# Traced rates for a build-time planner, sums placed later, and a 5x5 layer that alternates between sample and quarter-image inputs

## The chip, the cores and the metric

The kernel runs on one core of a Trainium2 chip. The metric is the device time of one execution in microseconds (us), given as the median of several runs. Engines are named as in the profile: PE (TensorE matmul), PEld (its weight loads), DVE (VectorE), ACT (ScalarE), POOL (GpSimd), SP (the queue that issues most DMAs).

## The reference, cut to what matters

Four layers, each `x = x + layer(groupnorm(x))`, on x of 16 samples, 32 channels, 128 x 128, float32.

```python
x = x + L0(_gn(x), ...)   # a row-skewed LSTM that scans over 128 columns
x = x + L1(_gn(x), w)     # quantised; out[f] = -sum over channels and 3x3 taps of |patch - w|
x = x + L2(_gn(x), w1)    # 2-D Hartley transform, 32x32 modes mixed over channels, transform back
x = x + L3(_gn(x), ...)   # U-net, below
# L3: five edge operators, each normalised per sample -> 160 channels
#   conv1 3x3 (160->32), maxpool2, conv2, maxpool2, conv3, maxpool2, conv4,
#   deconv1+conv5, deconv2+conv6, deconv3+conv7, times the input
```

In L1, 32 filters in 8 sets of 4, times 9 taps, are 72 differences for each half of each sample. In L3 the five operators and conv1 are folded into one 5x5 convolution whose weights depend on the sample's statistics.

## The kernel before, in words

**Stage 0** (to 687 us) is L0. It isn't changed.

**Stage 1** (687 to 5609 us) is L1, class `Differences`. It walks 16 samples x 2 halves, 32 units in all; each unit is 72 differences. One difference is either `nc.scalar.activation(Relu)` on ACT (L757, tile `d_act`, two buffers) or `nc.vector.tensor_scalar` on DVE (L760, tile `d_dve`, three buffers). PE then sums it over channels with 16 matmuls (`sums`, L647), tap by tap into four PSUM banks. `linear` (L662) adds nine more terms, `keep_busy` (L677) issues matmuls with zero weights where the plan has a gap, and `finish` (L628, L630) takes the unit out and its statistics.

**Behind it** the work of L2 and L3 is woven in. It runs on groups of four samples (class `After`): `forward` (transform, L1110 to L1082, then `mixing`, L1221), `back` (L1295, L1345), `statistics` (Gram products, L1487, and the operators' norms, L1555), the weights `wf` from tables `v` (L1610 to L1625), `conv1` (the sides, L1837, then eight chunks of 25 taps x 16 matmuls, L1863), `small_layers` (conv2, conv3, conv4, L1661; upsampling, `Composed.round`, L908 and L934), and `last`. Group g may start only when stage 1 has finished sample 4g+3.

**The order is made at build time.** `Weave` keeps a planned clock for PE, DVE and ACT. Each step of a generator yields its PE time in us; `yield SUMMED` waits until the plan has PE done with it, and `yield -x` waits x us. After every difference, `weave.advance(due)` issues background steps while they start before the next sum is due:

```python
            start = max(self.pe, self.ready)
            if start + 1.0 > due + SLACK:
                return
```

The planner also chooses ACT or DVE for each difference, and `keep_busy` fills what it thinks is left. `keep_order` then fixes this order on every engine; nothing is decided at run time. So a wrong price shows as an engine that waits, with all that stands behind it in its queue.

**The tail** (5609 to 6606 us): when the 72 x 32 differences are issued, `drain` runs what is left of the weave beside a second one for group 3. Group 3 keeps its image in SBUF (`whole`). `drain` steps whichever weave is behind in planned time.

**Layouts that the change touches.** In `conv1` a chunk is 16 image rows, `xp` of 20 rows with the halo; the four row tiles j of PE take four rows each (4j + kh). The output `y1` is `padded`: one image per channel. Each PE output bank holds, on partitions 32j to 32j+31, row tile j, so `spread` takes a bank out with four instructions of 32 partitions. A `quartered` tile holds a quarter of the image rows for each block of 32 partitions, so that `evict` takes a bank out with one instruction of 128 partitions; `neighbours` then copies the halo rows between the quarters.

## Time and profile before

| | |
|---|---|
| median of 3 runs | 6603.08 us (6602.0 to 6603.86) |
| the profiled execution: its time, its span | 6607.96 us, 6606.2 us |
| stage 0; stage 1; tail | 687 us; 4922 us; 997 us |
| busy over the span: PE, DVE, ACT | 81%, 84%, 82% |
| granted PE clock, mean | 0.919 |
| differences: on ACT, on DVE | 626 x 7148 ns, 1678 x 2360 ns |

The profile's groups give, for each line, engine and tile, the count, the busy time, the mean of one, and the idle time that its engine had just before it with what ended it. The windows give the busy time of every engine in a stretch, with the granted clock. In the profile each float32 matmul stands as two records, so that a 5x5 chunk of 400 matmuls is 800 records. A busy PE isn't one at its peak: ends of matmuls are modelled.

### The profile page before, as it was taken

The numbers are of one execution on the slowest core, as the hardware profiler recorded it, in microseconds if no ns is written. First come the engines' busy times: TensorE is split into PE (matmuls) and PEld (weight loads), VectorE is DVE, ScalarE is ACT, GpSimd is POOL, SyncE is SP. The second block draws the span as 40 slices with busy tenths as digits, with TensorE's granted clock in tenths as the row PEclk, the third lists the DMA queues.
The fourth block names the chain that finished last, engine by engine and source line by source line (L and its number), as shares of the span: only waits on it lengthen the run. The fifth ranks groups of instructions, "written<-read, shape, count | busy, mean of one in ns | idle before, by whom it ended". The sixth has DMA issues, their size and how long they took to land.

```text
span 6606.2 us, 269623 instructions
## 1 busy us (share of the span) xinstructions
PE 5331.0 (81%) x126486; PEld 2789.1 (42%) x126486; DVE 5543.3 (84%) x6844; ACT 5422.6 (82%) x3179; POOL 70.0 (1%) x67
## 2 busy tenths in 40 slices
PE   3798677788777879997887769998877779888796
PEld 3676233333334433333333433333333433445584
DVE  7898899999999989998899999999999999233322
ACT  3898899999999999998999989999999999112112
POOL 0000000000000000000000000000000000000000
PEclk9999899999998989998999889999999889987798
DMA  7553322221253632211553642121553641422302
GB/s 315 216 188 116 78 57 62 54 54 46 59 155 107 200 96 59 70 45 42 121 154 91 210 133 61 49 63 37 124 151 89 194 137 34 155 76 73 85 4 64
DMA packets 360800, 681.08 MB, mean 103 GB/s; under 512 B 71236, under 2 KB 219716, under 8 KB 348804
## 3 DMA queue, kind: packets, MB, share of 16 engines
q1 hardware_dynamic: 352212, 629.41, 33.3%
q0 software_dynamic: 7040, 33.80, 1.5%
q8 instruction: 989, 16.20, 1.0%
q14 instruction: 127, 1.04, 0.1%
q10 hardware_dynamic: 432, 0.64, 0.0%
HBM read 481.00 MB, written 182.69 MB: 100 GB/s over the span
## 4 chain that ended last, share of the span: by engine, by line
issue 33%; PE 29%; DVE 18%; ACT 15%; DMA 4%; SPq 1%; POOL 0%; DVEq 0%; ACTq 0%; POOLq 0%
PE acc L1863 11%; DVE d_dve L760 11%; ACT d_act L757 10%; PE acc L647 8%; PE pg L223 3%; PE acc L908 2%; PE acc L1661 2%; ACT gt L237 2%; DVE y L1768 1%; ACT junk L198 1%; DVE stat L124 1%; DMA xm_d<-xm 1%; DMA x_in<-in_x_dram 1%; DVE pooled L1757 1%; DMA v<-fold_d 1%
## 5 line engine op out<-in xcount | busy, mean ns | idle before, releaser
L757 ACT ACTIVATE d_act<-q,neg 128x8192 f16<-128x8192 f16 (+1 forms) x626 | 4428.1, 7148 | 159.2 <-PE acc L647 132.3
L760 DVE TENSOR_SCALAR d_dve<-q,qw 128x8192 f16<-128x8192 f16 (+1 forms) x1678 | 3871.1, 2360 | 174.4 <-PE acc L647 154.6
L647 PE MATMUL acc<-d_dve,sel 128*32 128x512 f16 x26848 | 1871.4, 401 | 445.5 <-DVE d_dve L760 346.8
L647 PEld LDWEIGHTS <-sel 128*32 128x32 f16 x36864 | 1003.6, 100 | 2088.2 <-issue 1416.4
L647 PE MATMUL acc<-d_act,sel 128*32 128x512 f16 x10016 | 728.0, 412 | 313.8 <-ACT d_act L757 299.3
L1863 PE MATMUL acc<-xp,wf 32*32 32x512 f32 x19200 | 757.3, 614 | 16.1 <-issue 12.9
L1771 ACT ACTIVATE y<-pooled,b 32x128 f32<-32x128 f32 x456 | 182.4, 400 | 429.9 <-DVE pooled L1757 423.7
L677 PE MATMUL acc<-q,zero 128*32 128x512 f16 x5676 | 407.2, 398 | 0.5 <-issue 0.5
L1863 PEld LDWEIGHTS acc<-xp,wf 32*32 32x32 f32 x19200 | 257.1, 104 | 324.9 <-issue 277.3
L223 PE MATMUL pg<-h,wb 64*64 64x20 f32 (+15 forms) x8192 | 345.9, 308 | 54.4 <-DVE h L251 29.5
L908 PE MATMUL acc<-y,u_conv 32*32 32x256 f32 (+1 forms) x9984 | 332.9, 447 | 68.0 <-issue 50.1
L237 ACT ACTIVATE gt<-pg,bias 128x20 f32<-128x20 f32 (+15 forms) x1024 | 332.7, 385 | 40.2 <-PE pg L223 37.8
L223 PEld LDWEIGHTS pg<-h,wb 64*64 64x64 f32 x8192 | 255.3, 153 | 129.9 <-DVE h L251 77.0
L677 PEld LDWEIGHTS <-zero 128*32 128x32 f16 x5676 | 169.6, 101 | 156.4 <-issue 31.5
L908 PEld LDWEIGHTS acc<-y,u_conv 32*32 32x32 f32 x9984 | 154.4, 109 | 190.7 <-issue 142.3
L1898 DVE TENSOR_TENSOR acc<-acc,cut 128x4 f32<-128x4 f32 x256 | 36.0, 164 | 227.8 <-PE acc L1863 225.3
L1863 PE MATMUL acc<-image,wf 32*32 32x512 f32 x6400 | 218.7, 599 | 0.6 <-issue 0.4
L223 PE MATMUL pg<-xn,wb 64*64 64x2 f32 (+63 forms) x4096 | 186.9, 293 | 25.5 <-issue 17.2
L1661 PE MATMUL acc<-y,w_conv 32*32 32x512 f32 (+2 forms) x4608 | 172.2, 528 | 37.0 <-issue 18.5
L1487 PE MATMUL acc<-xp 32*64 32x204 f32 (+2 forms) x6432 | 180.1, 337 | 26.1 <-issue 26.0
L1994 ACT ACTIVATE xr<-xr,l_ms 128x1024 f32<-128x1024 f32 x48 | 51.6, 1147 | 164.8 <-DVE xr L2024 110.8
L1863 PEld LDWEIGHTS acc<-image,wf 32*32 32x32 f32 x6400 | 169.7, 103 | 37.9 <-issue 8.7
(247 smaller groups left out, 3994.5 us busy)
## 6 DMA issues: line engine op xcount, KB each, us to landing
q<-q_d SPq DMA_DIRECT2D x128, 536.2 KB, 9.9
x_in<-in_x_dram SPq DMA_DIRECT2D x16, 2048.0 KB, 14.7
xn<-in_xs_dram SPq DMA_DIRECT2D x64, 512.0 KB, 7.1
res<-in_x_dram SPq DMA_DIRECT2D x64, 512.0 KB, 8.9
x_d<-res SPq DMA_DIRECT2D x64, 512.0 KB, 5.0
xq<-x_d SPq DMA_DIRECT2D x256, 128.0 KB, 4.1
xr<-x_d SPq DMA_DIRECT2D x256, 128.0 KB, 4.9
x_d<-xr SPq DMA_DIRECT2D x256, 128.0 KB, 2.6
```

The source lines that it names most:

```text
L124: nc.vector.bn_stats(stat0[:, g, 8 * q + k, :], t[:, k * 512 : (k + 1) * 512])
L223: nc.tensor.matmul(bank[c][q][64 * pair : 64 * pair + 64, :, :width], wb[half, 4 * kind + KIND[q]].rearrange("p b o -> p (b o)"), v[half], ...
L237: nc.scalar.activation(gt[:, q, :, :n], bank[c][q][:, :, :n], AF.Tanh if q == G else AF.Sigmoid, bias=bias[:, KIND[q] : KIND[q] + 1],)
L647: self.nc.tensor.matmul(acc[k][32 * j : 32 * j + 32, :], self.sel16[:, i // 9, :], d[:, row : row + 4, c : c + W], start=first, stop=last,)
L677: self.nc.tensor.matmul(acc[k][32 * j : 32 * j + 32, :], self.zero, q[:, :4, :W], start=False, stop=False)
L757: nc.scalar.activation(dst, src, AF.Relu, bias=self.neg[:, i : i + 1])
L760: nc.vector.tensor_scalar(dst, src, self.qw[:, i : i + 1], 0.0, ALU.subtract, ALU.max)
L908: nc.tensor.matmul(acc[blk][32 * j : 32 * j + 32, o : o + rows * n], t[part, 4 * par + tap, :], own[:, top : top + rows, left : left + n], ...
L1487: nc.tensor.matmul(gram[blk][j : j + width, at : at + n], xp[part, l, 2 + j : 2 + j + width], xp[part, rows, j : j + width + 4], start=sta ...
L1661: nc.tensor.matmul(acc[blk][32 * j : 32 * j + 32, : rows * n], wc[name][part, tap, :], src[part, at : at + rows, kw : kw + n], start=tap == 0,
L1771: nc.scalar.activation(d, s, AF.Identity, bias=bj)
L1863: nc.tensor.matmul(acc[blk][32 * j : 32 * j + 32, :], tap_of("all", tap)[rows], xp[rows, 4 * j + kh : 4 * j + kh + 4, kw : kw + W], start= ...
```

## The change

**Planner constants.** `PE_US` (one sum) 1.0 to 0.88, `SLACK` 3.0 to 1.0, a new `ACT_SPARE` of 1.5 us by which a sum of an ACT difference is placed later, the price of `linear` 0.45 to 0.36 and that of a `keep_busy` block 0.25 to 0.22. Every step's yield is set anew.

**Layout.** For groups 0 to 2 the 5x5 layer no longer reads the image chunk by chunk. `window(ch)` holds, for each of the four image quarters, eight rows starting at row 4 ch of that quarter; row tile j works in quarter j. The windows are loaded again from the padded image in DRAM, one DMA each. `y1` and `y3` become quartered, and conv1, conv2, conv3 and conv4 are taken out with one instruction per bank. Two additions for the image's left and right edge become one.

**Buffers.** Frames grow from 20 to 32 rows; to make room, the tables `gm` go from 5 to 3 buffers and `v` from 4 to 3 for groups 0 to 2, frames of the last weave from 4 to 3, and the DMA scratch from 4096 to 2048.

```diff
-DVE_US, ACT_US, PE_US = 2.36, 7.15, 1.0
-LATE = 1.5
-SLACK, CLOCK = 3.0, 1.0
+DVE_US, ACT_US, PE_US = 2.36, 7.15, 0.88
+LATE, ACT_SPARE = 1.5, 1.5
+SLACK, CLOCK = 1.0, 1.0
...
-        for k in range(min(int((until - start - 0.1) / 0.25), 4)):
+        for k in range(min(int((until - start - 0.1) / 0.22), 4)):
...
-                    unit["late"].append((ends[act], i, act, t))
+                    unit["late"].append((ends[act] + (ACT_SPARE if act else 0.0), i, act, t))
...
-            yield rows * n / 512 * 0.2 + 0.95        # Composed.round, one tap
+            yield rows * n / 512 * 0.78 + 0.28
...
-        self.buffers = {..., "frames": 2, "gm": 5, "e_v": 4, "l_x": 2}
+        self.buffers = {..., "frames": 2, "gm": 3, "e_v": 3, "l_x": 2}
...
-            yield 1.0                                # mixing
+            yield 0.3
             if ky % 4 == 3 and 8 < ky < M1 - 1 and not weave.draining:
-                yield -2.5
+                yield -5.5
...
-                    yield 1.1                        # back, first step
+                    yield 0.35
...
-                yield 0.8                            # back, second step
+                yield 0.4
...
-        ring = [pool.tile([128, 20, W + 4], F32, name=f"xp{i}") for i in range(self.buffers["frames"])]
+        ring = [pool.tile([128, 32, W + 4], F32, name=f"xp{i}") for i in range(self.buffers["frames"])]
...
-        def again(ch, half):
-            own = slice(10 * half, 10 * half + 10)
-            nc.sync.dma_start(chunk(ch)[:, own, :], padded(ch, own.start, own.stop))
+        def again(ch):
+            t = self.d["xn"]
+            rows = bass.AP(
+                t.tensor, t.offset + g * 128 * PADDED + 4 * ch * PW, [[PADDED, 128], [32 * PW, 4], [1, 8 * PW]]
+            )
+            nc.sync.dma_start(window(ch).rearrange("p (q r) w -> p q (r w)", q=4), rows)
...
-                yield 0.5                            # statistics, one row
+                yield 0.38
...
-            y1 = self.padded(y1p, 64, "y1")
+            y1 = self.quartered(y1p, 64, "y1")
...
-                            xp[rows, 4 * j + kh : 4 * j + kh + 4, kw : kw + W],
+                            xp[rows, at + apart * j + kh : at + apart * j + kh + 4, kw : kw + W],
...
-                yield 1.15                           # conv1, one tap
+                yield 1.06
...
-                for s, col in enumerate((0, W - 1)):
-                    nc.vector.tensor_tensor(a4[:, :, col], a4[:, :, col], cut[:, blk, s, ch, :], ALU.add)
+                nc.vector.tensor_tensor(sides_of, sides_of, both, ALU.add)
...
-                    self.spread(lambda part, j: y1[part, top + 2 * j : top + 2 * j + 2, 1:65], out[blk], blk, ...)
+                    self.evict(y1[:, blk, 1 + 2 * ch : 3 + 2 * ch, 1:65], out[blk], b1[:, blk : blk + 1], blk, nc.scalar)
+                if ch in (0, 7):
+                    self.neighbours(y1, 16, ch == 7, ch == 0)
...
-    nc = bacc.Bacc("TRN2", target_bir_lowering=False, num_devices=1, dynamic_dma_scratch_size=4096)
+    nc = bacc.Bacc("TRN2", target_bir_lowering=False, num_devices=1, dynamic_dma_scratch_size=2048)
```

Here `apart, at` are `8, 0` for a window and `32, 4 * ch` for the kept image of group 3. conv2 runs as two halves over the taps 3 to 8 and then 0 to 2, so that the halo rows from the last chunk are needed only for the last three.

## The prediction

> **What bounds the kernel now.** I read the page's head and slices first, then windows over the two stages that the change touches, then the waits inside stage 1, and last the groups, for prices.

> ```profile
> span 6606.2 us, 269623 instructions
> PE 5331.0 (81%) x126486; PEld 2789.1 (42%) x126486; DVE 5543.3 (84%) x6844; ACT 5422.6 (82%) x3179; POOL 70.0 (1%) x67
> ...
> DVE  7898899999999989998899999999999999233322
> ACT  3898899999999999998999989999999999112112
> ```

> The page's rows for DVE and ACT fall from 9 to 2 at slice 35. Up to there the kernel is stage 1; behind it is another machine. The windows price both:

> ```profile
> 687.00:5609.00 4922.00, 4041.58 (x88090) 1870.70 (x88091) 4677.28 (x3941) 4745.19 (x1180) 59.63 (x45) 0.93 0.35 94
> 5609.00:6607.00 998.00, 818.67 (x26105) 537.45 (x26087) 304.02 (x853) 163.10 (x327) 7.94 (x15) 0.87 0.27 76
> ```

> Columns: length, busy time of PE, PEld, DVE, ACT, POOL, then granted clock, DMA share and GB/s. In stage 1 DVE and ACT are busy 95% and 96%; less work on both, or less waiting, is what shortens it. In the tail PE is busy 82%, DVE 30%: PE and the chain of waits bound it. A second cut shows what PE does there:

> ```profile
> 5612.00:6250.00 638.00, 515.55 (x15566) 297.83 (x15564) 214.09 (x595) 92.76 (x187) 7.94 (x15) 0.83 0.35 98
> 6250.00:6607.00 357.00, 300.12 (x10473) 238.52 (x10468) 89.44 (x258) 67.45 (x134) 0.00 (x0) 0.93 0.14 38
> ```

> At 6250 group 2's last matmul is done; group 3 runs alone after it. The same windows for line L1863 alone (PE, PEld, clock, DMA):

> ```profile
> 5612.00:5887.00 275.00, 190.31 (x4704) 78.28 (x4704) 0.91 0.46 136
> 6250.00:6432.00 182.00, 181.84 (x5568) 151.78 (x5564) 1.00 0.06 16
> ```

> A chunk is 800 records. So six chunks of group 2's conv1 lie in the tail before 5887, and alone a chunk costs 182/5568 x 800 = 26.1 us. In the waits of stage 1 the sums (L647) and the differences wait for each other:

> ```profile
> PE acc L647 <- DVE d_dve L760: 346.8, 318, 10.3
> PE acc L647 <- ACT d_act L757: 299.3, 185, 6.1
> PEld acc L1863 <- issue: 223.9, 533, 3.1
> DVE d_dve L760 <- PE acc L647: 154.6, 115, 8.6
> ACT d_act L757 <- PE acc L647: 132.3, 47, 19.8
> ```

> The two last rows cost time: 155 us of DVE and 132 us of ACT, because PE had not yet freed a buffer. PE's own waiting costs nothing by itself, but a sum that waits for ACT holds the DVE sums queued behind it.

> [...] its clock has only two values, and one sum's 16 matmuls, which take 1.05 us at 1154 us, take 1.90 us at 1165.9, after PE had waited 2.54 us; the mean in stage 1 is 0.93. [...] a DVE take-out that is placed too early blocks the differences behind it, as `ta` (L1114) does here, up to 5.25 us.

> **The change part by part.** Counts come from the two programs' orders of instructions, durations from the groups of this execution.

> *1. The layout takes work off ACT and DVE in stage 1.* ACT: 280 take-outs of 32 partitions go, 88 of 128 come. [...] L1771's 400 ns agrees. So -280 x 0.40 + 88 x 0.40 = -77 us. The planner gives ACT 631 differences for 626: +5 x 7.15 = +36. ACT's sum: **-41 us**. DVE: 128 take-outs of conv2 to conv4 become 32, -96 x 0.275 = -26; 144 edge additions of 164 ns become 88, -9; 16 more poolings (0.66) +11; 27 halo copies at 0.2 (estimate, from 128x16 copies of 0.175 and 128x128 of 0.284) +5; five differences fewer, -12. DVE's sum: **-31 us**. These lie on the engines that set stage 1, so it can shorten by 30 to 40 us.

> *2. The background runs ahead.* Cheaper yields let `advance` issue more between two sums. In units of 72 differences, the order of before starts group 2's transform at unit 27.2 and its conv1 at 31.0; the order after at 26.0 and 29.1. At the end 2400 of its conv1 matmuls (six chunks) lay behind the last difference, afterwards 511 (1.28): **4.72 chunks leave the tail**. The price of before, 1.15 us a tap, was above the 1.05 that the lone chunk shows; 1.06 is true. PE pays for them in stage 1, 4.72 x 26.1 = 123 us, and for 2908 more zero matmuls, at most 157 us (16 per 0.86 us); it was busy 82% there, so 90% after. Nothing on DVE or ACT is added by this beyond part 1.

> *3. What the tail saves.* If PE alone counted: 123 us, 150 where the chunks shared PE (275 us for 5.88 chunks, with other work between). If group 3's waits alone counted: nothing. So I went through group 3 by steps, taking from the trace each step's own PE time and waits, and from the order after what is left of group 2 to fill them. Start to first transform: 51 us before, 45 after. Transform 55, 45. Wait for modes and mixing 94, 53 (14 us of PE idle is before it now; conv2 and conv3 cover it). Trip through z and L1295: 81, 55. L1345: 71, 55. Statistics' lead 37, 35. Statistics up to group 2's new end 60 and their rest, alone, 45 (125 in all before). Weights 38, 38. Sides 34, 20. These are 586 before and 451 after. Conv1 from there: 238 before (its first chunk shared PE with group 2), 217 after. What follows it, 170 before: four take-outs, each shorter by 1 to 2 us, give 164. Sum: 994 to 832, -162. I take **-150 us**, since less filler means more half clock (0.56 already at 6150 to 6200) and waits that I can't see. Range -100 to -175.

> *4. Waiting in stage 1.* SLACK 1.0 lets a background step make a sum late by one step, where before it was three us; with three buffers DVE has 2 x 2.36 - 0.88 = 3.8 us before it notices. ACT's sums placed 1.5 us later spare PE part of the 299 us; the ACT buffer still has 7.15 - 1.5 - 0.88 us to spare. More zeros hold the clock: 118 of the 220 us that DVE idles lie at half-clock stretches. Against it, the true rates leave no margin when the clock halves, and take-outs come due earlier. I take **-35 us**, between -120 and +70.

> *5. Fewer table buffers.* With `v` at 3 and `gm` at 3, a reload is issued after a use and needed three uses later. [...] here `v` lands in 6.9 us (median) and `gm` in 7.2, so the trace's numbers are used. `v` is used every 1.4 us where steps come in a row, so perhaps one wait of 4 us in each group; `gm` is used every 2.6 us, so one of 3 us. DVE would hold the differences behind it. Three groups: **+20 us**, 0 to 60 (the smaller DMA scratch, which no row prices, is in the upper end).

> *6. At nothing.* Window loads: 24 of 2.1 MB for 48 of 0.66 MB. A load of 2 MB lands in 14.7 us (x_in), and a chunk lasts 65 us of stage 1 (0.42 units of 154 us), so two windows cover it. In the tail a chunk lasts 26 us: still covered. q, xq and xr queue behind it on SP, with about 20 us of lead each. The layout of conv matmuls: same counts and shapes.

> **Sum.** -31 (DVE's side) - 150 - 35 + 20 = -196 us: 6606 to about 6410 for a profiled span. The median of the runs stands 3 us below that span: **6407 us**.

> **Rivals.** *Hidden gain lost:* late take-outs and table waits eat part 1 and 4, and only the tail shortens, less the table waits; 6603 - 150 + 20 = 6473; 0.18. For it: the removed price margin. Against it: PE still has about 10%. *Waits vanish:* DVE idles 100 us instead of 220, 6407 - 90 = 6317; 0.12. For it: up to 1500 us DVE idles next to nothing (2 us of 313 in 687 to 1000), as zeros alone fill PE there. *The tail doesn't shrink:* group 3's chain sets it, -30 there, 6527; 0.05. Against it: PE at 515 of 638 us. *Slower:* PE becomes the bound of stage 1. If the half clock meets the denser order, sums fall behind by more than the 3.8 us of buffers, DVE and ACT stand, and each of the 24 units that carry background grows. The gain of 150 + 31 is used up at 7.5 us a unit (5%); at 9 us the time is 6603 - 181 + 216 = 6638; 0.06. For it: the conv1 stretch goes from 3.71 to 3.41 units in group 0. Against it: that stretch runs at clock 0.95 to 0.98, PE's own work there is near 90%. That the change doesn't do what it says is excluded for the order, not for its effect.

> **How the numbers follow.** The likeliest case has 0.59, about 6360 to 6450. With the rivals, 6315 to 6510 leaves out 2 in 10. 0.2% (13 us) is about what a measurement of this kernel can tell from no change: the tail's case splits 0.03 to faster and 0.02 to same, so faster 0.59 + 0.18 + 0.12 + 0.03 = 0.92, same 0.02, slower 0.06.

> **What the new profile would show.** Last difference at 5540 to 5600 us, tail of 830 to 880 us; under 1100 records of conv1's `xp` after it; L1771's group at a quarter of its instructions, still about 400 ns; waits of d_dve for L647 under 155 us; granted clock of stage 1 at or over 0.93. I am wrong if stage 1 ends after 5609, or if PE's share of the tail drops below 75%, which would mean that waits took the place of the chunks.

## The result, and the profile after

The changed kernel takes **6502.38 us** (median of four runs, 6494.89 to 6506.94), the kernel before 6603.47 us beside it on the same chip: ratio 0.9845, interval 0.9828 to 0.9862. That is 101 us faster, about half of the 196 us that the prediction's sum gave. The time lies inside the range of 6315 to 6510 us that the prediction named, 8 us from its upper end, and outside its likeliest case of 6360 to 6450. That was luck in part: the range was wide because of the rivals, and the sum that it was built around was off by a factor of two. The profiled execution took 6506.94 us with a span of 6505.2; the one of before has 6606.2, so the two spans differ by 101 us too and can be compared piece by piece.

The head, the slices and the chain of work that ended last, from the page of the changed kernel:

```profile
span 6505.2 us, 274662 instructions
PE 5343.1 (82%) x129394; PEld 2805.1 (43%) x129394; DVE 5475.0 (84%) x6551; ACT 5312.8 (82%) x2816; POOL 65.6 (1%) x67
...
DVE  7799899999999999999999889999989889744212
ACT  3899799999999989999999899999989899702001
...
PE 41%; issue 25%; DVE 20%; ACT 8%; DMA 4%; SPq 1%; POOL 0%; DVEq 0%; ACTq 0%; POOLq 0%
```

DVE and ACT have lost 68 and 110 us of work over the whole span, as the layout should bring. But between slices 22 and 33 DVE's row now has five 8s and ACT's three, where those of before have none and one. PE's share of the last chain is 41%; before it was 29%. Work went off DVE and ACT, and PE has become what they wait for more often.

Windows over stage 1 and the tail of the changed kernel (length, busy time of PE, PEld, DVE, ACT and POOL, granted clock, DMA share, GB/s):

```profile
691.00:5646.00 4955.00, 4224.36 (x94756) 1948.29 (x94757) 4654.82 (x3827) 4708.23 (x999) 55.25 (x45) 0.94 0.36 99
5646.00:6506.00 860.00, 651.62 (x22340) 478.61 (x22336) 258.17 (x673) 90.50 (x144) 7.97 (x15) 0.83 0.30 81
```

Length less busy time gives idle time. The tail is 138 us shorter (998 to 860). Stage 1 is 33 us **longer** (4922 to 4955), although DVE is busy 22 us less in it (4677 to 4655) and ACT 37 us less (4745 to 4708): DVE's idle time rose from 245 to 300 us, ACT's from 177 to 247. Stage 0, which is unchanged, took 4 us more in this execution. So 4 + 33 - 138 = -101.

The waits in stage 1 of the changed kernel (total us, times, longest):

```profile
PE acc L647 <- DVE d_dve L760: 333.6, 327, 31.3
...
DVE d_dve L760 <- PE acc L647: 195.1, 191, 10.6
ACT d_act L757 <- PE acc L647: 190.1, 86, 13.1
PE acc L647 <- ACT d_act L757: 142.4, 100, 4.5
```

Before, these read 346.8, 154.6, 132.3 and 299.3. PE waits 157 us less for ACT, and DVE and ACT wait 98 us more for PE. Read together, the two say that PE runs later than it did; the prediction took the first half of that as a gain and missed the second.

Two stretches of 450 us show some of where. First the kernel before, in group 1's conv1 and then in group 2's transform, mixing, transform back and statistics:

```profile
4000.00:4450.00 450.00, 432.29 (x9528) 166.33 (x9524) 426.46 (x286) 438.98 (x175) 0.00 (x0) 0.97 0.23 62
4900.00:5350.00 450.00, 351.29 (x8128) 187.92 (x8116) 430.70 (x373) 446.43 (x110) 15.00 (x9) 0.91 0.51 146
```

The corresponding stretches of the changed kernel lie 150 us earlier:

```profile
3850.00:4300.00 450.00, 432.98 (x9869) 162.23 (x9862) 428.96 (x266) 434.43 (x94) 0.00 (x0) 0.99 0.25 70
4750.00:5200.00 450.00, 350.71 (x8708) 189.55 (x8700) 401.42 (x417) 407.56 (x111) 17.56 (x15) 0.89 0.53 159
```

In group 1's conv1 PE is busy 96% of the stretch, and DVE idles no longer than before (24 us, then 21). In the other stretch PE is busy 78% in both kernels, and DVE's idle time goes from 19 to 49 us, ACT's from 4 to 42.

These two don't stand for the whole of stage 1. In the changed kernel group 2's conv1 fills its last 416 us; there PE is busy 97% and DVE idles 28 us:

```profile
5230.00:5646.00 416.00, 404.62 (x9374) 158.44 (x9368) 388.42 (x224) 397.69 (x79) 0.00 (x0) 0.99 0.20 57
```

Cut into pieces of 50 us (mean over five places of the cuts), the pieces of stage 1 in which PE is busy 93% or more hold 56 us of DVE's idle time before and 87 us after. So about half of the 55 us lies where PE is fullest, and the rest where it has time free. Little of it lies at half clock: 94 us of DVE's idle time fell there before, 102 after.

### The profile page after: what moved, and what is told of

The parts are those of the page before. It is cut to its first block, busy times and chain, and to the rows that moved or that the text cites. A ratio compares the mean times of both kernels' runs of the same rounds, so it can differ in the third digit from the quotient of the medians.

```text
span 6505.2 us, 274662 instructions
## 1 busy us (share of the span) xinstructions
PE 5343.1 (82%) x129394; PEld 2805.1 (43%) x129394; DVE 5475.0 (84%) x6551; ACT 5312.8 (82%) x2816; POOL 65.6 (1%) x67
## 4 chain that ended last, share of the span: by engine, by line
PE 41%; issue 25%; DVE 20%; ACT 8%; DMA 4%; SPq 1%; POOL 0%; DVEq 0%; ACTq 0%; POOLq 0%
PE acc L647 14%; PE acc L1874 13%; DVE d_dve L760 12%; ACT d_act L757 4%; PE acc L908 3%; PE pg L223 3%; ACT gt L237 2%; PE acc L1664 2%; ACT junk L198 1%; PE acc L1491 1%; PE acc L677 1%; DVE stat L124 1%; PE acc L662 1%; DMA v<-fold_d 1%; PE acc L1221 1%
## 5 line engine op out<-in xcount | busy, mean ns | idle before, releaser
L757 ACT ACTIVATE d_act<-q,neg 128x8192 f16<-128x8192 f16 (+1 forms) x631 | 4470.2, 7149 | 209.1 <-PE acc L647 190.1
L760 DVE TENSOR_SCALAR d_dve<-q,qw 128x8192 f16<-128x8192 f16 (+1 forms) x1673 | 3866.9, 2360 | 215.7 <-PE acc L647 195.1
L647 PE MATMUL acc<-d_dve,sel 128*32 128x512 f16 x26768 | 1862.5, 397 | 429.2 <-DVE d_dve L760 333.6
L647 PEld LDWEIGHTS <-sel 128*32 128x32 f16 x36864 | 984.7, 99 | 1968.1 <-issue 1291.7
L647 PE MATMUL acc<-d_act,sel 128*32 128x512 f16 x10096 | 713.7, 403 | 153.3 <-ACT d_act L757 142.4
L1874 PE MATMUL acc<-xp,wf 32*32 32x512 f32 x19200 | 721.1, 609 | 16.7 <-issue 15.8
L677 PE MATMUL acc<-q,zero 128*32 128x512 f16 x8584 | 582.7, 388 | 6.3 <-issue 6.3
L1874 PEld LDWEIGHTS acc<-xp,wf 32*32 32x32 f32 x19200 | 225.2, 103 | 315.9 <-issue 285.8
L908 PE MATMUL acc<-y,u_conv 32*32 32x256 f32 (+1 forms) x9984 | 313.0, 461 | 50.8 <-issue 33.8
L677 PEld LDWEIGHTS <-zero 128*32 128x32 f16 x8584 | 247.3, 99 | 229.3 <-issue 35.2
L1792 ACT ACTIVATE y<-pooled,b 128x128 f32<-128x128 f32 x112 | 39.7, 396 | 348.9 <-DVE pooled L1767 230.7
L1874 PE MATMUL acc<-image,wf 32*32 32x512 f32 x6400 | 207.3, 605 | 0.0
L1874 PEld LDWEIGHTS acc<-image,wf 32*32 32x32 f32 x6400 | 180.5, 103 | 24.1 <-issue 3.5
L1908 DVE TENSOR_TENSOR acc<-acc,cut 128x8 f32<-128x8 f32 x128 | 19.5, 166 | 194.0 <-PE acc L1874 194.0
L1664 PE MATMUL acc<-y,w_conv 32*32 32x512 f32 (+2 forms) x4608 | 142.7, 476 | 26.5 <-issue 19.0
## 6 DMA issues: line engine op xcount, KB each, us to landing
x_in<-in_x_dram SPq DMA_DIRECT2D x16, 2048.0 KB, 14.7
```

The lines of the kernel that those rows point to most:

```text
L647: self.nc.tensor.matmul(acc[k][32 * j : 32 * j + 32, :], self.sel16[:, i // 9, :], d[:, row : row + 4, c : c + W], start=first, stop=last,)
L677: self.nc.tensor.matmul(acc[k][32 * j : 32 * j + 32, :], self.zero, q[:, :4, :W], start=False, stop=False)
L757: nc.scalar.activation(dst, src, AF.Relu, bias=self.neg[:, i : i + 1])
L760: nc.vector.tensor_scalar(dst, src, self.qw[:, i : i + 1], 0.0, ALU.subtract, ALU.max)
L908: nc.tensor.matmul(acc[blk][32 * j : 32 * j + 32, o : o + rows * n], t[part, 4 * par + tap, :], own[:, top : top + rows, left : left + n], ...
L1664: nc.tensor.matmul(acc[blk][32 * j : 32 * j + 32, : rows * n], wc[name][part, tap, :], pick(part, blk, j)[:, tap // 3 : tap // 3 + rows, t ...
```

## The experiments

Each run is given as its ratio to the kernel before, taken on the same chip. Idle time is stage 1's length less DVE's busy time in it. "Left" counts group 2's conv1 matmuls that the order puts behind the last difference (400 are one chunk; the profile shows two records for each). Stage 1 runs from the first to the last difference.

| kernel | left | stage 1 | DVE idle there | tail | ratio (interval) |
|---|---|---|---|---|---|
| before | 2400 | 4922 | 245 | 998 | 1 |
| after | 511 | 4955 | 300 | 860 | 0.9845 (0.9828-0.9862) |
| e1_layout | 2831 | 4861 | 241 | 1017 | 0.9942 (0.9927-0.9957) |
| e2_planner | 80 | 5024 | 310 | 856 | 0.9944 (0.9928-0.9961) |
| e3_spare0 | 0 | 4996 | 342 | 845 | 0.9864 (0.9849-0.9879) |
| e4_slack3 | 0 | 5277 | 563 | 714 | 1.0105 (1.0090-1.0120) |
| e5_small | 2895 | 4882 | 246 | 1017 | 0.9950 (0.9933-0.9967) |
| e6_zeros6 | 511 | 4930 | 277 | 861 | 0.9801 (0.9783-0.9818) |
| e7_small55 | 1439 | 4889 | 242 | 919 | 0.9833 (0.9812-0.9854) |
| e8_s55z6 | 1439 | 4866 | 221 | 923 | 0.9823 (0.9808-0.9837) |
| e9_s55z10 | 1439 | 4865 | 221 | 915 | 0.9804 (0.9788-0.9821) |
| e10_s55z6k15 | 0 | 5008 | 332 | 798 | 0.9847 (0.9829-0.9865) |
| e11_zeros10 | 511 | 4935 | 283 | 850 | 0.9799 (0.9782-0.9816) |
| e12_s55z10k12 | 671 | 4933 | 276 | 865 | 0.9811 (0.9791-0.9831) |

**The two halves of the change alone.** e1_layout is the changed kernel with all of the planner's numbers set back to those of before:

```diff
-DVE_US, ACT_US, PE_US = 2.36, 7.15, 0.88
-LATE, ACT_SPARE = 1.5, 1.5
-SLACK, CLOCK = 1.0, 1.0
+DVE_US, ACT_US, PE_US = 2.36, 7.15, 1.0
+LATE, ACT_SPARE = 1.5, 0.0
+SLACK, CLOCK = 3.0, 1.0
...
-            yield 0.3
+            yield 1.0
```

The last pair is mixing; the other yields go back to those of before in the same way.

> The changed layout and buffers with every planner constant of before (SLACK 3, no ACT_SPARE, old prices of sums, zeros and background steps). 2831 conv1 matmuls lie behind the last difference (2400 before). Theory A (the planner's new numbers cause the added waiting of stage 1): DVE idle near 220 us, stage 1 about 30 us shorter than before (4890), tail about 1010: 6570 to 6590. Rival B (the layout or the fewer table buffers cause the waiting): stage 1 at 4950 or over, 6620 to 6640.

e2_planner is the opposite: the kernel before, with its layout and buffers, and the new numbers in all these places.

> The layout of before with all new planner constants. 80 conv1 matmuls are left behind the last difference. Theory A: stage 1 has DVE idle of 280 or more and ends about 30 us later than in the changed kernel (no work is taken off DVE and ACT), near 4990, tail 850 to 870: 6520 to 6545. Rival B: DVE idle near 220, stage 1 about 4930, 6470.

Windows of stage 1 and tail, first e1_layout, then e2_planner:

```profile
689.00:5550.00 4861.00, 3988.11 (x87290) 1841.23 (x87293) 4620.14 (x3773) 4713.69 (x978) 57.81 (x45) 0.93 0.36 98
5550.00:6567.00 1017.00, 833.48 (x27124) 525.47 (x27112) 276.74 (x718) 103.15 (x174) 7.95 (x15) 0.89 0.29 82
```

```profile
688.00:5712.00 5024.00, 4281.79 (x95238) 1967.60 (x95253) 4713.92 (x4006) 4758.70 (x1269) 67.59 (x45) 0.94 0.35 93
5712.00:6568.00 856.00, 643.14 (x21536) 492.67 (x21504) 290.42 (x801) 122.08 (x224) 7.95 (x15) 0.81 0.30 82
```

The layout alone is worth 0.58%, 38 us: stage 1 is 61 us shorter, all of it DVE's busy time (4677 to 4620) with idle time as before, and the tail 19 us longer, since 2831 conv1 matmuls wait for it instead of 2400. The planner's numbers alone are worth 39 us: the tail is 142 us shorter and stage 1 is 102 us longer, 65 of them idle time of DVE and 37 work that came with the background. So the added waiting belongs to the planner's numbers, not to the layout, its windows or its fewer buffers. Together the two give 1.55%, more than 0.58 + 0.56; why was not looked into.

**Which of the planner's numbers make PE late.** e3_spare0 takes back the later place of ACT's sums (`ACT_SPARE` 0.0 for 1.5), e4_slack3 the limit on lateness (`SLACK` 3.0 for 1.0); all else is the changed kernel.

> The changed kernel with ACT_SPARE 0 instead of 1.5. Theory A1 (sums of ACT placed 1.5 us later hold ACT's buffers and cause the growth of ACT's waits for L647 from 132 to 190 us): ACT waits back under 150 us, PE's waits for d_act back to about 300 us, time 6470 to 6490. Rival A2 (the spare pays): DVE and ACT both wait more, since a sum that waits for ACT blocks the DVE sums behind it: 6520 to 6550.

> The changed kernel with SLACK 3.0 instead of 1.0: a background step may make a sum late by three us. All of group 2's conv1 then lies before the last difference. If lateness against DVE's three buffers is what the waits come from: d_dve and d_act wait for L647 over 480 us in all (385 in the changed kernel), stage 1 over 5000 us, tail about 40 us shorter (820): 6530 to 6560. If waits come from half clock and not from planned lateness: stage 1 as in the changed kernel, tail shorter: 6460.

Waits in stage 1 of e4_slack3:

```profile
DVE d_dve L760 <- PE acc L647: 406.0, 262, 10.2
...
ACT d_act L757 <- PE acc L647: 375.3, 161, 13.4
```

With 3 us of allowed lateness at the new rates the two waits are twice those of the changed kernel. All of conv1 that can leave the tail leaves it (714 us), and the kernel is slower than before, 1.0105. So at the new rates more allowed lateness turns into waiting on DVE and ACT: this is shown for 3 us against 1. It also lets more work into stage 1: PE's work in the tail falls from 652 to 484 us. No run goes below 1.0, so how much of the changed kernel's own waiting comes from its 1.0 is not shown. At the old rates the same 3 us did no such harm (e1_layout: 149.4 and 97.6 us). That the old prices were too high and held back the time that the slack gave away is the likely reason; it was only argued.

`ACT_SPARE` pays a little, as the rival in its expectation said. Without it the two waits rise to 221 and 206 us and DVE idles 42 us more, though the order then also leaves no conv1 for the tail. But PE's wait for ACT rises only from 142.4 to 166.2 us, so most of the fall from 299 is not its doing. The medians differ by 21 us in its favour, on different chips, and the intervals of the ratios overlap.

**The steps of many small matmuls.** PE has waits that nothing in the program explains, ended by "issue"; the last section shows what they are. In stage 1 they add up to 145 us before and 206 after. Lines of three background steps from PE's waits in stage 1, before, then after:

```profile
PE acc L1295 <- issue: 9.1, 7, 2.7
...
PE acc L1837 <- issue: 8.9, 9, 2.3
PE acc L1221 <- issue: 2.9, 3, 1.4
```

```profile
PE acc L1295 <- issue: 34.0, 17, 7.1
...
PE acc L1221 <- issue: 21.9, 14, 2.4
PE acc L1847 <- issue: 21.5, 11, 8.7
```

These are the transform back, the sides (L1837 before, L1847 after) and mixing: 21 us before, 77 after. The timeline of the changed kernel shows one case (start, duration, what, and in brackets the idle time before it and what ended it):

```profile
4842.76 1.09 PE L1295 MATMUL acc<-cw,zi 32*32 32x32 f32 x104
...
4845.17 1.36 PE L1295 MATMUL acc<-cw,zi 32*32 32x32 f32 x128 [1.32 <-issue]
...
4848.64 1.54 PE L1295 MATMUL acc<-cw,zi 32*32 32x32 f32 x128 [2.11 <-issue]
...
4852.66 1.54 PE L1295 MATMUL acc<-cw,zi 32*32 32x32 f32 x128 [2.48 <-issue]
...
4861.06 0.39 PE L1295 MATMUL acc<-cw,zi 32*32 32x32 f32 x24 [6.87 <-issue]
...
4861.39 3.60 PE L647 MATMUL acc<-d_dve,sel 128*32 128x512 f16 x32
...
4863.34 2.35 DVE L760 TENSOR_SCALAR d_dve<-q,qw 128x8192 f16<-128x8192 f16 x1 [10.62 <-PE acc L647]
...
4866.79 7.13 ACT L757 ACTIVATE d_act<-q,neg 128x8192 f16<-128x8192 f16 x1 [13.06 <-PE acc L647]
```

One matmul on float32 shows as two records (conv1's 9600 on `xp` are the 19200 of L1874), so a step of 16 is 32 records, and these 512 are 16 steps, planned at 0.35 us each: 5.6 us. While they run, they run at that rate (104 records in 1.09 us, 10.5 ns each, 0.34 us a step), but PE stands still 12.8 us between bursts of 128 records, and the whole takes 18.7 us, 1.17 a step. Over the three groups of stage 1 the stalls of L1295 are 34.0 us for 96 steps, another 0.35 us a step. Then the sums that stood behind run at half clock, 32 matmuls in 3.60 us, where 16 take 1.04 us at 4867.36, at full clock again. The granted clock is 0.50 from 4846.0 to 4866.5 us, so it had fallen before the stall of 6.87 us. DVE stands 10.6 us and ACT 13.1. So 0.35 is the price of a burst, and such a step also costs its stalls; the price of before, 1.1, had room for them.

e5_small sets the prices of mixing, of back's first step and of the sides to those of before (1.0 with a pause of 2.5 for 5.5, 1.1 and 0.6). e7_small55 sets them between:

```diff
-            yield 0.3
+            yield 0.5
...
-                    yield 0.35
+                    yield 0.55
...
-                yield 0.35
+                yield 0.5
```

> The changed kernel with the old prices of three steps of many small matmuls alone: mixing 1.0 (and its wait 2.5), the first step of back 1.1, the sides 0.6. 2895 conv1 matmuls lie behind the last difference (511 in the changed kernel). Theory C (at their burst price these steps run PE out of instructions; PE idled 77 us before L1295, L1221 and L1847 with nothing to wait for, 21 us before the change, and the sums queued behind them came late): that idle falls to 35 us or less, DVE idles in stage 1 about 265 us instead of 316, stage 1 is 70 to 100 us shorter (also for the chunks it no longer holds), the tail 150 us longer: 6550 to 6590. Rival D (half clock and denser sums cause the waiting, not these steps): DVE idle stays at 300 or over, 6600 or more.

> As e5 with prices between: mixing 0.5, first step of back 0.55, sides 0.5. 1439 conv1 matmuls are left behind the last difference. Theory C: PE's idle before the three steps near 50 us, DVE idle of stage 1 near 290 us; stage 1 about 45 us shorter than in the changed kernel, tail about 60 us longer: 6500 to 6530. Rival D: stage 1 shorter only by the moved work (10 us), 6550.

PE's waits in stage 1 of e7_small55, the same steps:

```profile
PE acc L1847 <- issue: 11.0, 10, 1.8
...
PE acc L1295 <- issue: 8.7, 10, 2.2
PE acc L1221 <- issue: 8.4, 6, 2.4
```

And the stretch from transform to statistics, by the same window as in the changed kernel:

```profile
4750.00:5200.00 450.00, 367.60 (x8856) 200.15 (x8848) 424.30 (x392) 430.39 (x113) 9.59 (x7) 0.93 0.53 156
```

The stalls of these steps fall from 77 to 28 us (all of this kind from 206 to 176), the longest from 8.7 to 2.4, and DVE's idle time in this stretch from 49 to 26. In all of stage 1 the waits of `d_dve` and `d_act` are 149.3 and 121.0 us, the level of before. But the total hardly moves (0.9833 against 0.9845, overlapping intervals): at higher prices the background gets less far, 1439 conv1 matmuls are left for 511, and the tail is 59 us longer.

e5_small goes further. With only these prices (and the pause) of before, the stalls of the three steps are 15.5 us and the waits 149.9 and 123.9, but 2895 matmuls are left, the tail is 1017 us and the ratio that of the layout alone. So the other new rates alone don't carry conv1 out of the tail; it takes the prices of these short steps, with the pause, and the same prices make PE stall.

That such a stall makes DVE and ACT wait is seen in the timeline above. How much of the added waiting is the stalls' own is not shown by these two runs, because the same prices also keep work out of stage 1; a run further down speaks to that.

**The zero matmuls.** `keep_busy` fills PE until 0.1 us before the next sum is due by plan. When PE is late, a zero matmul takes time in which it could have caught up: in the changed kernel 8584 of them are 582.7 us of PE's busy time. e6_zeros6 stops 0.6 us ahead, e11_zeros10 1.0 us:

```diff
-        for k in range(min(int((until - start - 0.1) / 0.22), 4)):
+        for k in range(min(int((until - start - 0.6) / 0.22), 4)):
```

> The changed kernel with a keep_busy that stops 0.6 us before the next sum is due instead of 0.1: 5280 zero matmuls instead of 8584, every other instruction in the same order. Rival E (zeros fill PE so full that it can't catch up after being late): DVE idle in stage 1 falls from 316 to 260 us, time 6450. Theory C or D: the half-clock time of stage 1 rises from 567 us, idle stays or grows, time 6500 to 6560.

> The changed kernel with zeros that stop 1.0 us before the sum, all prices as changed: as in the kernel whose zeros stop at 0.6 us, with fewer of them. If the gap for catching up counts: DVE idle in stage 1 at 280 us or less (316 in the changed kernel, 293 with zeros to 0.6 us), 6465 to 6478. If 0.6 us was enough and the clock now suffers: half-clock time of stage 1 over 700 us and 6485 to 6510.

Groups of the page of the changed kernel, then of e11_zeros10 (count | busy us, mean ns | idle before, releaser):

```profile
L760 DVE TENSOR_SCALAR d_dve<-q,qw 128x8192 f16<-128x8192 f16 (+1 forms) x1673 | 3866.9, 2360 | 215.7 <-PE acc L647 195.1
...
L677 PE MATMUL acc<-q,zero 128*32 128x512 f16 x8584 | 582.7, 388 | 6.3 <-issue 6.3
```

```profile
L760 DVE TENSOR_SCALAR d_dve<-q,qw 128x8192 f16<-128x8192 f16 (+1 forms) x1673 | 3864.6, 2360 | 200.6 <-PE acc L647 180.7
...
L677 PE MATMUL acc<-q,zero 128*32 128x512 f16 x2156 | 200.2, 403 | 0.0
```

The order is otherwise the same, with 511 matmuls left. (The expectations' 316 and 293 us of DVE idle stand 16 us above the count in the table.) With 3304 zeros fewer (e6) the medians fall by 25 us, with 6428 fewer by 28 us; both intervals lie below that of the changed kernel. In the profiles, stage 1 is 25 and 20 us shorter and DVE idles 23 and 17 us less, under half of the 56 us that the expectation of e6 gave to this cause; the rest lies in stage 0, which is the same program and took 7 and 4 us less, and in e11's tail (10 us less). The stalls ended by "issue" don't shrink with the zeros (206 us, then 193 and 210), so it is not fewer instructions that help. The time at half clock, from the granted-clock records between 700 us and the last difference, is 567 us in the changed kernel, 618 in e6 and 727 in e11, as much as in the kernel before (730): the zeros do hold the clock, and what they hold is worth less here than the gaps that they take. (That a sum which starts on time at half clock, 1.90 us, still keeps ahead of a DVE difference of 2.36 us is the likely reason; it was only argued.)

**Both, and more lateness on top.** e8_s55z6 and e9_s55z10 join the prices of e7_small55 with zeros that stop 0.6 and 1.0 us ahead; e10_s55z6k15 and e12_s55z10k12 are these two with `SLACK` 1.5 (and 0.6 for the first step back) and 1.2.

> The small steps' middle prices (mixing 0.5, first step of back 0.55, sides 0.5) together with zero matmuls that stop 0.6 us before the sum. If the two causes of lateness are separate (small steps without instructions, and no gap to catch up): the gain of 24 us that the zeros gave alone is added, stage 1 about 4865, tail 920: 6475. If it is one cause seen twice: 6495 to 6500, as with the prices alone.

> As e8, but zeros stop 1.0 us before the sum: 2200 of them (5252 in e8), every other instruction in the same order. If zeros are still worth having for the clock: half-clock time of stage 1 well over 620 us, waiting grows, 6490 to 6520. If catching up is worth more: 6455 to 6470.

> As e8 with SLACK 1.5 and 0.6 for the first step of back; no conv1 matmul of group 2 is left behind the last difference (1439 in e8). If half a microsecond more of planned lateness is within DVE's three buffers: stage 1 longer only by the work it takes on (15 us), tail 80 us shorter: 6410 to 6430. If lateness costs as SLACK 3.0 did (176 us over 2 us): stage 1 longer by 60 us, 6460 to 6480.

> The small steps' middle prices, zeros that stop 1.0 us before the sum, SLACK 1.2 instead of 1.0. 671 conv1 matmuls are left behind the last difference (1439 at SLACK 1.0), so the tail is 45 to 50 us shorter, near 868. If the waiting grows with SLACK evenly (113 us of DVE idle for 0.5): +45 us there, no gain, 6465 to 6475. If most of the growth lies above 1.2: 6430 to 6450.

The waits go below those of the kernel before (e9: 128.7 and 110.2 us; DVE idle 221), but in the total no gain over fewer zeros alone can be told: e9 stands at 0.9804, e11 at 0.9799, e6 at 0.9801, not to be told apart. More slack moves more conv1 out of the tail and gives it back in stage 1: from e9 to e12 the tail loses 50 us and stage 1 gains 68, from e8 to e10 125 and 142. From e7 to after, with "left" going from 1439 to 511, the exchange was about even (tail -59, stage 1 +66), and from after to e4 it lost most (-146, +322). The medians of e12 against e9 (6483.79, 6468.53) and of e10 against e8 (6493.65, 6481.85) point the same way, with intervals of the ratios that overlap; both e10 and e12 came out slower than either of the cases that their expectations named.

e12 also bears on the stalls. Its small steps are spaced as in e7_small55, and their stalls are 35 us against 82 in e11_zeros10, which differs from it in these prices and in `SLACK`. Yet its waits of `d_dve` and `d_act`, 179.0 and 161.1 us, are about those of e11, 180.7 and 169.5, once 0.2 us more of slack has brought conv1 nearly as far (671 matmuls left, 511 in e11). So the low waiting of e7 came in part from the work that it kept out of stage 1, and the stalls are one cause of PE's lateness, whose share is open.

e6, e9 and e11 are faster than both kernels, e9 with the lowest median at 6468.53 us. Which of them is best is open.

## Why the prediction was right or wrong

- **Step 1, right within 9 us; step 2, right in the count.** DVE and ACT were to lose 31 and 41 us in stage 1; they lost 22 and 37. With the layout alone DVE loses 57. Of the 35 us that came back, 19 moved out of the tail with the chunks (DVE's work there is 258 us after and 277 in e1_layout), so "nothing on DVE or ACT is added by this" was 19 us off; 15 more lie in the differences, three more of which went to DVE. The prediction gave the tap's price as the reason for the earlier conv1. e5_small keeps the new tap price and still leaves 2895 matmuls: it takes the prices of three short steps and the pause. The 90% that PE should be busy does not follow from the step's own sum (82% and 280 us more of 4922 are 88%); measured is 85%.
- **Step 3, right.** -150 forecast, -138 measured, and a tail of 860 us in the forecast 830 to 880. PE's share of it is 652 of 860, 76%, above the 75% that would have refuted it. The step's own figure of 150 us for chunks that share PE follows from the 190 us that PE is busy with them, not from the 275 us named beside it. Behind 5646 us lie 960 records of conv1 on `xp` (7360 of L1874, less 6400 on group 3's image), under the forecast 1100.
- **Step 4, wrong, and most of the miss.** Waiting was to shrink by 35 us; DVE's idle time grew by 55, table waits included, inside the step's range of -120 to +70. e1_layout and e2_planner show that the planner's new numbers brought it. The step had seen both signs ("the true rates leave no margin") and gave the wrong one more weight. Of its three grounds, `ACT_SPARE` helped, but by little. `SLACK` 1.0 is a smaller number than 3.0, but it doesn't mean less lateness where the prices have no margin: raising it costs waiting at once (e4, e10, e12). And more zeros hold the clock, from 730 us at half clock to 567, but DVE's idle time at half clock did not fall with it (94 us, then 102), and the zeros take the gaps in which PE could catch up. The step counted 220 us of idle time, of which 118 in half-clock stretches; the windows that it shows give 245, and the clock records put 94 of them at half clock. What the step did not know at all is that a step of small matmuls, priced at its burst rate, stalls PE for up to 8.7 us.
- **Step 5, mis-sized.** 20 us for fewer table buffers; measured are 6.3 us of waits for `v` (7.8 before) and 3.5 for `gm` (none before), about 2 us more:

```profile
DVE wf L1630 <- DMA v<-fold_d: 6.3, 8, 2.6
```

- **Step 6, right.** A window load of 2.1 MB lands in 9.0 us (median), below the 14.7 taken for it, and no wait of conv1 for it stands out. The 0.40 us of a take-out in step 1 are L1771's 400 ns for 32 partitions; that 128 would take no longer was the author's estimate. The take-outs on ACT came as priced, 112 of 396 ns:

```profile
L1792 ACT ACTIVATE y<-pooled,b 128x128 f32<-128x128 f32 x112 | 39.7, 396 | 348.9 <-DVE pooled L1767 230.7
```

The miss adds up: 9 us of work, 12 of the tail, 70 of steps 4 and 5 together (-15 forecast, +55 measured) and 4 of stage 0 make 95, the distance from -196 to -101. Of the marks named for the new profile, the tail, the records, L1771's successor (L1792) and the clock (0.94) came out; the last difference (5540 to 5600 forecast, 5646 measured) and the wait for L647 (under 155, 195 measured) did not. The prediction's own test, that it is wrong if stage 1 ends after 5609, caught this. The nearest rival in kind is the hidden gain lost, at 6473, though what ate the gain was a late PE (planned lateness, zeros, stalls) and not table waits. "The tail doesn't shrink", at 6527, is as near in time but not what happened, since the tail shrank by 138 us. "Waits vanish" did not come either; its 6317 would be 6322 by its own terms, 120 us of waiting less the 35 already counted. The slower rival put the danger in conv1, where PE is fullest. In group 1's conv1 nothing was lost, but about half of the added waiting lies where PE is 93% busy or more, so it saw part of the truth. That sums can fall behind by more than the buffers hold is real: e4_slack3 shows it, with 406 and 375 us of waits of `d_dve` and `d_act`. The sum at 1165.9 us in the kernel before shows that the clock halves (its records hold 1.0 and 0.5 alone: 1.0 up to 1165.2 us, 0.5 from there to 1172.1), but what length of wait brings that was not shown.

## What to carry to other kernels

When an order is fixed at build time, the wait of the consumer for PE and the wait of PE for the producer have to be read together: a fall in one that comes with a rise in the other is a shift in time and not a gain. A price taken from a burst is not the price of a step (0.34 us against 1.17 in the timeline here); include the stalls around it. A run that changes a price also changes how far the background gets, so compare it with one that gets as far. And filler that protects a clock should stop early enough that a late engine can catch up, which one run with less filler tells (here the medians fell by 25 us with 3304 zeros fewer).

## What the runs showed of the hardware

PE can stand still for want of instructions. In the timeline above, after 128 records of small matmuls and their 128 weight loads, issued in 1.4 to 1.5 us, it stalled for 2.1 to 6.9 us, three times in a row. One of the page's rows for queues that bring instructions, before and then after:

```profile
q8 instruction: 989, 16.20, 1.0%
```

```profile
q8 instruction: 1012, 16.58, 1.1%
```

- When PE's instructions are numbered in order, 68 of the 73 stalls of over 1 us that "issue" ended stand at the same place modulo 256, within six neighbouring numbers. Of the 163 other waits of that length, no six neighbouring numbers hold more than 8.
- 66 of the 73 end 1.1 to 1.7 us after a packet of this queue has landed; of the other waits 9 in 163 do.

The four stalls of the timeline are among them: by the packet records, blocks landed at 4843.89, 4847.25, 4851.29 and 4859.43 us, and PE went on 1.3 to 1.6 us after each. So these stalls are waits for the next 256 instructions. The spacing of e7_small55, which shortens them, agrees with it. What held up the packet before the longest stall, which started 5.4 us after PE had gone on, is open; that it stood behind other transfers was not tested.

Half clock cost less here than the filler against it: e11_zeros10 spends 160 us more of stage 1 at half clock than the changed kernel and is 28 us faster. What half clock costs by itself was not measured.
